# A graph layer with experts: projected rows kept as float32 and split into float32r parts on chip

## The chip, the cores and the metric

One core of a Trainium2 chip runs the whole program. The metric is device time in microseconds (us), the median of three runs. PE is the matrix engine (PEld its weight loads), DVE the vector engine, ACT the scalar engine, POOL GpSimd, SP the engine that issues most DMA transfers. Each engine takes its instructions in the order of the program that was built; engines wait for one another and for transfers by semaphores.

## What is computed

There are 6250 rows of 256 numbers and 100000 edges (`src`, `dst`), sorted by `dst`. The edges are stacked as (src, dst), so a row's neighbours are the `dst` of the edges that have it as `src`. Cut to what matters here:

```python
xn = layernorm(x)
agg = segment_sum(xn[dst], src); cnt = segment_sum(1, src)
gnn = xn @ W1.T + b1 + (agg / max(cnt, 1)) @ W2.T + b2
x = x + gnn + mix(xn)            # mix: products within 8 heads, plus xn
x = x + ffn(layernorm(x))        # each row goes to one of 8 experts
```

Since the sum over neighbours is linear, the kernel projects first, z = xn @ W2.T, and sums rows of z. This sum is the heaviest part, and the change is about how z is kept.

## The kernel before, in words

Products on PE are done in float32r, a form of float32 with fewer bits. To keep the precision, each row of z is held as two float32r parts, a high part and the remainder, and each is multiplied by itself into the same sum. Both parts are stored side by side in the DRAM tensor `z_d`: 512 numbers, 2 KB a row.

*First stage, to about 290 us.* DVE sorts the edges by `src` in many short steps (`step`, `pairs`, `last_steps`), with PE turning the data at some of them. Beside it runs `mixer`, a generator whose pieces `tick` puts between the steps of the sort, by fixed weights (`MIX`, `OWN`). For each of 49 tiles of 128 rows, a piece normalises the rows on ACT (L393), turns the next tile (L400), multiplies by `w2s` into `pz` (L421), copies the high part to `zr` as float32r (L426), multiplies it by minus one into the same `pz` so that the remainder is left there (L429), copies that to the second half of `zr` (L433), and has SP store the tile in `z_d` (L434). `zr` has three buffers. On every second tile from the seventh on, `segment` has SP load a pair of tiles of `z_d` into `z_s` (L385), twelve pairs in all. They are rows near the `dst` of each of twelve segments of the edges, and stay on chip. SP's queue thus holds stores of `z_d`, loads of `z_s` and loads of x in the order of the program.

*Second stage, from 290 us to about 1040 us.* A loop over 49 blocks `b` of 128 rows sums neighbours in `pa`. Two kinds of edges are summed:
- near edges: for each of 24 tiles of `z_s`, PE counts on chip how often a row is a neighbour (`counts`, L920: four products into `pc`), ACT casts the counts to `cn` (L923), and PE multiplies them by the tile in `z_s`. The one-hot operands `on` and `od` are made by DVE two blocks ahead (`hot_classes`, L894). Counts are two sets of four ahead of their use, and `pc` has two buffers.
- other edges, up to 1152 a block, in nine tiles of 128: POOL gathers their rows of z from `z_d` by an indirect DMA each (L910), into one of 19 buffers `zb`, and PE multiplies them by the one-hot `og`, which DVE makes a block ahead (L900). A gather into a buffer waits until PE has used it.

`add_rows` does two products each time (L823, L824): the remainder with two columns of ones, which count the edges, and the high part. A block has six steps `q`, each with four tiles of `z_s` and one or two gathered tiles; at its end `meaned` reads the sum (L970), and after every seventh block `gate_pieces` puts the gate's work in pieces between the following steps: normalising (L993), turning (L1000), `hT` (L1003), logits (L1008), choice of expert, ranks (L1043), places (L1090). It also has SP store seven tiles of rows in `buf_d` (L1074, 1.8 MB) and in `out` (L1096, 0.9 MB). Each block also loads its own x (`xt`) and y by ACT's queue and `ov` by SP's; DVE adds x and y into `row` (L960, L963). `lane_w`, an operand of L894 and L900, lies in PSUM.

*Third stage, to the end.* The experts' products (L1281, L1290), almost without a pause on PE.

There is also a loop over all edges in order (L831 on), for edges that don't fit; its number of rounds is computed, and it is zero here.

The two products, and the loop's schedule of gathered tiles:

```python
nc.tensor.matmul(ps[:, :AW], lhsT, z[:, D:], start=first, stop=False, skip_group_check=True)
nc.tensor.matmul(ps[:, :D], lhsT, z[:, :D], start=False, stop=last, skip_group_check=True)
...
t1 = GT * (j0 + 4) // J0 if j0 + 4 < J0 else GT
if not b:
    t1 = (0, 0, 2, 4, 7, GT)[q]
for t in range(t0, t1):
    add_rows(pa, og[:, t, :], zb[(b * GT + t) % NZ], not begun, False)
```

Of the kernel before, what the change touches and what calls it, by code (L numbers as in the profile page):

```python
# [16 lines left out]
P = 128  # L17
N = 6250
D = 256
NT = 49  # L20
# [3 lines left out]
DZ = 2 * D  # L24
DW = DZ + 2
# [11 lines left out]
ND = 12  # L37
# [3 lines left out]
NW = 2 * P  # L41
# [7 lines left out]
NB = NT  # L49


J0 = 2 * ND
GT = 9
# [7 lines left out]
NEC = 125  # L61
# [13 lines left out]
EPS = 1e-5  # L75
NZ = 19
OWN = 0.4
# [10 lines left out]
def gnn_mix_moe_kernel(ctx: ExitStack, tc: tile.TileContext, x, src, dst, w1t, b1g, w2t, b2g,  # L88
                       kw, kb, vw, vb, gate_w, gate_b, fw1, fb1, fw2, fb2, out):
    nc = tc.nc  # L90

    dram = ctx.enter_context(tc.tile_pool(name="dram", bufs=1, space=bass.MemoryType.DRAM))
    z_d = dram.tile([NT * P, DZ], F32, name="z_d")
    y_d = dram.tile([NT * P, D], F32, name="y_d")
# [15 lines left out]
    minus = const.tile([P, P], F32R, name="minus")  # L110
    nc.vector.tensor_scalar(minus, ident, -1.0, None, op0=OP.mult)
    ones_b = const.tile([P, P], BF16, name="ones_b")
# [50 lines left out]
    zs_ = ExitStack()  # L163
    z_p = zs_.enter_context(tc.tile_pool(name="z", bufs=1))
    z_s = z_p.tile([P, J0, DW], F32R, name="z_s")

# [11 lines left out]
    with tc.tile_pool(name="early", bufs=1) as ep, tc.tile_pool(name="work", bufs=2) as wp, \  # L178
# [199 lines left out]
        xTa = ep.tile([P, NT, 2, P], F32, name="xTa")  # L378

        def segment(i):  # L380

            _, offs = nc.values_load_multi_w_load_instructions(
                nr[0:1, i:i + 1], engines=[ET.SP], min_val=0, max_val=P if not i else NW,
                skip_runtime_bounds_check_because="it is kept in bounds")
            nc.sync.dma_start(z_s.bitcast(F32)[:, 2 * i:2 * i + 2, :DZ],  # L385
                              z_d[lo_n[i]:NW * i + 3 * P][bass.ds(offs[0], NW), :].rearrange("(j p) d -> p j d", p=P))

        def mixer():
# [19 lines left out]
            for tt in range(NT):  # L408
# [26 lines left out]
                if tt >= 6 and not tt % 2 and tt // 2 - 3 < ND:  # L435
                    segment(tt // 2 - 3)
# [392 lines left out]
    with tc.tile_pool(name="over", bufs=1) as op, \  # L829
            tc.tile_pool(name="ops", bufs=1, space=bass.MemoryType.PSUM) as pp:  # L830
        with tc.For_i(0, nit) as i:  # L831
# [12 lines left out]
            nc.vector.memset(zo.bitcast(F32)[:, DZ:], 1.0)  # L844
            nc.gpsimd.indirect_dma_start(out=zo.bitcast(F32)[:, :DZ], out_offset=None, in_=z_d,
                                         in_offset=bass.IndirectOffsetOnAxis(ap=ngb, axis=0))
            po = pp.tile([NEC, AW], F32, name="po")
            add_rows(po, eqo, zo, True, True)
# [18 lines left out]
    with tc.tile_pool(name="gather", bufs=1) as ap_, tc.tile_pool(name="gwork", bufs=2) as wp, \  # L867
# [6 lines left out]
        nc.vector.tensor_copy(lane_w, lane_b.bitcast(I32))  # L874

        zb = []
        for i in range(NZ):
            zt = ap_.tile([P, DW], F32R, name=f"zb{i}")
            nc.gpsimd.memset(zt.bitcast(F32)[:, DZ:], 1.0)
            zb.append(zt)  # L880
# [21 lines left out]

        asked, used = 0, 0

        def gathers():

            nonlocal asked
            while asked < min(used + NZ, NB * GT):
                b, t = divmod(asked, GT)
                nc.gpsimd.indirect_dma_start(  # L910
                    out=zb[asked % NZ].bitcast(F32)[:, :DZ], out_offset=None, in_=z_d,
                    in_offset=bass.IndirectOffsetOnAxis(ap=idx[:, t, b:b + 1], axis=0))
                asked += 1

        def counts(b, j0):
# [202 lines left out]

# [269 lines left out]
```

## Time and profile before

| | |
|---|---|
| median of three runs | 1362.95 us (1360.56 to 1372.96) |
| the profiled execution: its time, its span | 1377.47 us, 1375.5 us |
| busy: PE, DVE, POOL, ACT | 1108.2, 751.6, 528.9, 437.6 us |
| mean granted PE clock | 0.924 |
| DMA | 269.12 MB, mean 196 GB/s |
| of it by POOL's queue (gathers and scatters) | 134.11 MB, 31.2% of 16 engines' span |
| gathers L910 | 441, 961 ns each on POOL, 292.2 to 988.2 us |
| first and last L970 | 332.3 us, 1009.5 us |

A profile is one execution, and its durations belong to that execution, not to the median. A group's row names the line, the engine, the operation, output<-inputs, the number, then busy us and the mean ns of one, then the idle time before it and what ended most of that. A window's row gives the busy time of each engine in a stretch, with the number of instructions, the share of full clock that PE was granted, the busy share of the 16 DMA engines and GB/s. A wait row names who waited for whom. "issue" is time in which the engine waited for nothing that the profile shows.

### The profile page before, as it was taken

The page shows a single profiled execution, that of the slowest core. Times are in us where ns is not written, and L with a number is a line of the kernel's source. Part 1 is how long each engine was busy: PE and PEld are TensorE (multiplying, and loading weights), DVE is VectorE, ACT ScalarE, POOL GpSimd, SP SyncE. Part 2 cuts the span into 40 slices and gives each one's busy share as a digit, 9 for nine tenths or more (in the row PEclk, how much of TensorE's full clock was granted, in tenths as well). Part 3 has the DMA queues.
Part 4 walks back from the last instruction along what each step waited for, and adds up shares of the span by engine and source line. Part 5 has one row for each costly group of instructions (what it writes and reads, how often), then busy time and mean ns, then how long its engine had stood idle before and what let it go on. Part 6 is the DMA issues. An engine that isn't in the chain of part 4 may idle for free.

```text
span 1375.5 us, 20920 instructions
## 1 busy us (share of the span) xinstructions
PE 1108.2 (81%) x7417; PEld 995.8 (72%) x7417; DVE 751.6 (55%) x2202; ACT 437.6 (32%) x960; POOL 528.9 (38%) x580
## 2 busy tenths in 40 slices
PE   0688968736779878878789779879848999999997
PEld 0477756535778777778778778768846888888886
DVE  8998776742745554554654644544561343433434
ACT  0566833401223223323323223222432322223221
POOL 0000002046665565566666565656401222322221
PEclk9999988966999989999989989989978999999999
DMA  8665213256876886776876875865755676666750
GB/s 242 209 227 189 92 52 107 90 176 195 275 223 202 182 265 197 203 259 207 225 247 195 236 220 166 235 205 172 201 156 202 221 243 212 216 216 209 247 189 21
DMA packets 147421, 269.12 MB, mean 196 GB/s; under 512 B 18947, under 2 KB 92365, under 8 KB 147308
## 3 DMA queue, kind: packets, MB, share of 16 engines
q0 software_dynamic: 41664, 134.11, 31.2%
q1 hardware_dynamic: 75431, 105.44, 25.4%
q10 hardware_dynamic: 30213, 28.15, 6.8%
q8 instruction: 60, 0.98, 0.3%
q14 instruction: 53, 0.43, 0.1%
HBM read 216.33 MB, written 51.82 MB: 195 GB/s over the span
## 4 chain that ended last, share of the span: by engine, by line
PE 62%; issue 5%; DVE 5%; DMA 3%; another core or an unknown queue 3%; ACT 1%; POOL 0%; ACTq 0%; DVEq 0%; POOLq 0%
PE pa L823 15%; PE pa L824 13%; PE pu L1281 12%; PE pd L1290 11%; PE pc L920 7%; DMA buf_d<-row 2%; PE lgr L1008 2%; PE ph L1000 1%; ACT cn L923 1%; PE pB L1269 1%; DVE on L894 1%; DMA bt<-buf_d,idx_s 1%; DVE row L974 0%; DVE og L900 0%
## 5 line engine op out<-in xcount | busy, mean ns | idle before, releaser
L910 POOL DMA_INDIRECT zb<-z_d,idx x441 | 423.8, 961 | 273.8 <-issue 95.0
L823 PE MATMUL pa<-z_s,cn 128*128 128x258 f32 x1176 | 348.8, 324 | 12.4 <-issue 11.8
L824 PE MATMUL pa<-z_s,cn 128*128 128x256 f32 x1176 | 318.7, 298 | 13.1 <-issue 13.0
L923 ACT CAST cn<-pc 128x512 fp32r<-128x512 f32 x294 | 171.4, 586 | 445.0 <-PE pc L920 153.3
L823 PEld LDWEIGHTS pa<-z_s,cn 128*128 128x128 f32 x1176 | 242.7, 206 | 18.6 <-issue 17.9
L824 PEld LDWEIGHTS pa<-z_s,cn 128*128 128x128 f32 x1176 | 242.6, 206 | 13.9 <-issue 13.9
L894 DVE TENSOR_TENSOR on<-lane_w,nvl 128x1024 bf16<-128x1024 bf16 x147 | 101.0, 687 | 238.7 <-PE pc L920 93.3
L920 PE MATMUL pc<-od,on 128*128 128x128 bf16 x1176 | 125.7, 232 | 56.0 <-issue 31.6
L1282 ACT ACTIVATE hm<-pu,b1e 128x256 f32<-128x256 f32 (+1 forms) x192 | 88.3, 460 | 246.8 <-PE pu L1281 221.4
L1281 PE MATMUL pu<-bT,w1e 128*128 128x256 f32 (+1 forms) x768 | 163.1, 371 | 0.0
L1290 PE MATMUL pd<-w2e,hm 128*128 128x256 f32 x720 | 163.0, 379 | 0.0
L1281 PEld LDWEIGHTS pu<-bT,w1e 128*128 128x128 f32 x768 | 138.3, 192 | 24.1 <-issue 7.3
L1290 PEld LDWEIGHTS pd<-w2e,hm 128*128 128x128 f32 x720 | 134.8, 190 | 17.2
L1304 POOL DMA_INDIRECT out_dram<-lim,tki_s x45 | 45.3, 1007 | 238.8 <-DVE lim L1303 227.9
L823 PE MATMUL pa<-zb,og 128*128 128x258 f32 x441 | 129.8, 307 | 8.3 <-issue 8.2
L920 PEld LDWEIGHTS <-on 128*128 128x128 bf16 x1176 | 76.3, 103 | 76.1 <-issue 54.4
L824 PE MATMUL pa<-zb,og 128*128 128x256 f32 x441 | 124.8, 295 | 6.5 <-issue 6.4
L1293 DVE TENSOR_TENSOR yt<-pd,b2e 128x256 f32<-128x256 f32 x45 | 19.1, 424 | 180.9 <-PE pd L1290 167.4
L824 PEld LDWEIGHTS pa<-zb,og 128*128 128x128 f32 x441 | 90.3, 205 | 10.2 <-issue 10.1
L823 PEld LDWEIGHTS pa<-zb,og 128*128 128x128 f32 x441 | 90.5, 205 | 6.8 <-issue 6.7
L589 POOL DMA_INDIRECT kb<-srt_d,bi x5 | 5.2, 1043 | 204.3 <-DVE bi L585 203.1
L421 PE MATMUL pz<-w2s,xTa 128*128 128x256 f32 x196 | 56.8, 412 | 15.0 <-ACT xTa L432 14.4
(405 smaller groups left out, 1486.3 us busy)
## 6 DMA issues: line engine op xcount, KB each, us to landing
w1e<-in_fw_dram SPq DMA_DIRECT2D x24, 1024.0 KB
w2e<-in_fw_dram SPq DMA_DIRECT2D x24, 1024.0 KB
z_d<-zr SPq DMA_DIRECT2D x49, 256.0 KB
buf_d<-row SPq DMA_DIRECT2D x6, 1795.5 KB
zb<-z_d,idx POOLq DMA_INDIRECT x441
ovf_d<-zero ACTq DMA_DIRECT2D x1, 6321.0 KB
ov<-ovf_d SPq DMA_DIRECT2D x49, 129.0 KB
y_d<-xg ACTq DMA_DIRECT2D x7, 896.0 KB
```

The lines of the kernel that those rows point to most:

```text
L421: nc.tensor.matmul(pz, xT[:, c, :], w2s[:, c, :], start=(c == 0), stop=(c == 1))
L823: nc.tensor.matmul(ps[:, :AW], lhsT, z[:, D:], start=first, stop=False, skip_group_check=True)
L824: nc.tensor.matmul(ps[:, :D], lhsT, z[:, :D], start=False, stop=last, skip_group_check=True)
L894: nc.vector.tensor_tensor(to[b % 2][:, c, :].rearrange("p c (m j) -> p c m j", j=2), lanes[:, None, :w].to_broadcast([P, n, w, 2]), of.to_ ...
L910: nc.gpsimd.indirect_dma_start(out=zb[asked % NZ].bitcast(F32)[:, :DZ], out_offset=None, in_=z_d, in_offset=bass.IndirectOffsetOnAxis(ap=i ...
L920: nc.tensor.matmul(pc[:, j - j0, :], on[:, j // 2, (j % 2) * P:(j % 2 + 1) * P], od[:, j // 2, :], start=True, stop=True, skip_group_check ...
L923: nc.scalar.copy(cn[:, :n, :], pc[:, :n, :])
L1008: nc.tensor.matmul(lgp[:, t, :], hT[:, c, :], gw[:, c, :], start=(c == 0), stop=(c == 1), skip_group_check=True)
L1281: nc.tensor.matmul(pu, w1e[:, c, f * P:(f + 1) * P], bT[:, c, :q], start=(c == 0), stop=(c == 1))
L1282: nc.scalar.activation(hms[s][:, f, :q], pu, AF.Relu, bias=b1e[:, f:f + 1])
L1290: nc.tensor.matmul(pd, hm[:, f, j * P:(j + 1) * P], w2e[:, f, :], start=(f == 0), stop=(f == FC - 1))
L1304: st = nc.gpsimd.indirect_dma_start(out=out, out_offset=bass.IndirectOffsetOnAxis(ap=tki_s[:, c:c + 1], axis=0), in_=lim, in_offset=None, ...
```

## The change

z is stored as plain float32: `z_d` has 256 numbers a row, 1 KB. The projection copies `pz` once, as float32, and the product with `minus` and the second copy are gone. A new helper `in_parts` makes the two parts on chip: ACT copies to float32r (the high part), and DVE subtracts that from the float32 rows and writes the remainder.

It is used in two places. The twelve pairs of near rows are loaded to one buffer `zw`, and are split into `z_s` at the next call of `segment`, ahead of the next load. The gathers go to seven buffers `zg` of three tiles each, and each group of three is split by one ACT copy and one DVE subtraction of 768 numbers a partition, into one of three buffers `zb`. Two groups are split ahead of the loop; then one more after each group that PE has used, and the gathers that this frees are asked for. The gathered tiles are multiplied three at a time, at every second step of a block. The loop for edges that don't fit gets the same split.

```diff
+GS = 3
+NZ = 7
+NQ = 3
...
-    z_d = dram.tile([NT * P, DZ], F32, name="z_d")
+    z_d = dram.tile([NT * P, D], F32, name="z_d")
...
+    def in_parts(to, z):
+
+        nc.scalar.copy(to[:, :, :D], z)
+        nc.vector.tensor_tensor(to[:, :, D:DZ], z, to.bitcast(F32)[:, :, :D], op=OP.subtract)
...
         def segment(i):

+            while loaded:
+                n, zw = loaded.pop()
+                in_parts(z_s[:, 2 * n:2 * n + 2, :], zw)
+            if i == ND:
+                return
...
-            nc.sync.dma_start(z_s.bitcast(F32)[:, 2 * i:2 * i + 2, :DZ],
-                              z_d[lo_n[i]:NW * i + 3 * P][bass.ds(offs[0], NW), :].rearrange("(j p) d -> p j d", p=P))
+            zw = wp.tile([P, 2, D], F32, name="zw", bufs=1)
+            nc.sync.dma_start(zw, z_d[lo_n[i]:NW * i + 3 * P][bass.ds(offs[0], NW), :].rearrange(
+                "(j p) d -> p j d", p=P))
+            loaded.append((i, zw))
...
-                zr = wp.tile([P, DZ], F32R, name="zr", bufs=3)
-                nc.scalar.copy(zr[:, :D], pz)
+                zr = wp.tile([P, D], F32, name="zr", bufs=3)
+                nc.scalar.copy(zr, pz)
                 if more:
                     pT = turned(tt + 1, xn)
-                nc.tensor.matmul(pz, minus, zr[:, :D], start=False, stop=True, skip_group_check=True)
                 nc.scalar.copy(u[:, 2 * t:2 * t + 2, :], pu)
                 if more:
                     nc.scalar.copy(xTa[:, tt + 1], pT)
-                nc.scalar.copy(zr[:, D:DZ], pz)
-                nc.sync.dma_start(z_d[tt * P:(tt + 1) * P, :], zr.bitcast(F32))
-                if tt >= 6 and not tt % 2 and tt // 2 - 3 < ND:
+                nc.sync.dma_start(z_d[tt * P:(tt + 1) * P, :], zr)
+                if tt >= 6 and not tt % 2 and tt // 2 - 3 <= ND:
                     segment(tt // 2 - 3)
...
+        zg = [ap_.tile([P, GS, D], F32, name=f"zg{i}") for i in range(NZ)]
...
-            while asked < min(used + NZ, NB * GT):
+            while asked < min((parted + NZ) * GS, NB * GT):
                 b, t = divmod(asked, GT)
                 nc.gpsimd.indirect_dma_start(
-                    out=zb[asked % NZ].bitcast(F32)[:, :DZ], out_offset=None, in_=z_d,
+                    out=zg[asked // GS % NZ][:, asked % GS, :], out_offset=None, in_=z_d,
                     in_offset=bass.IndirectOffsetOnAxis(ap=idx[:, t, b:b + 1], axis=0))
                 asked += 1
+
+        def split():
+
+            nonlocal parted
+            if parted * GS < NB * GT:
+                in_parts(zb[parted % NQ], zg[parted % NZ])
+                parted += 1
+                gathers()
...
+        for _ in range(NQ - 1):
+            split()
...
-                t1 = GT * (j0 + 4) // J0 if j0 + 4 < J0 else GT
-                if not b:
-                    t1 = (0, 0, 2, 4, 7, GT)[q]
+                t1 = (((q + 1) // 2) if b else max(0, q - 2)) * GS
                 for t in range(t0, t1):
-                    add_rows(pa, og[:, t, :], zb[(b * GT + t) % NZ], not begun, False)
+                    n = b * GT + t
+                    add_rows(pa, og[:, t, :], zb[n // GS % NQ][:, n % GS, :], not begun, False)
                     begun = True
+                if t1 > t0:
+                    split()
                 t0 = t1
-                used = b * GT + t1
-                gathers()
```

More of the change, by code (lines that the diff above doesn't have):

```diff
@@ L75 @@
 EPS = 1e-5
-NZ = 19
+GS = 3
+NZ = 7
+NQ = 3
 OWN = 0.4
@@ L109, in gnn_mix_moe_kernel @@
     nc.vector.tensor_scalar(before, jp, 0.0, None, op0=OP.is_gt)
-    minus = const.tile([P, P], F32R, name="minus")
-    nc.vector.tensor_scalar(minus, ident, -1.0, None, op0=OP.mult)
     ones_b = const.tile([P, P], BF16, name="ones_b")
@@ L378, in gnn_mix_moe_kernel @@
         xTa = ep.tile([P, NT, 2, P], F32, name="xTa")
+        loaded = []
         def segment(i):
+            while loaded:
[3 more added lines that the diff above has]
+                return
             _, offs = nc.values_load_multi_w_load_instructions(
@@ L844, in gnn_mix_moe_kernel @@
             nc.vector.memset(zo.bitcast(F32)[:, DZ:], 1.0)
-            nc.gpsimd.indirect_dma_start(out=zo.bitcast(F32)[:, :DZ], out_offset=None, in_=z_d,
+            zr = op.tile([NEC, D], F32, name="zr")
+            nc.gpsimd.indirect_dma_start(out=zr, out_offset=None, in_=z_d,
                                          in_offset=bass.IndirectOffsetOnAxis(ap=ngb, axis=0))
+            nc.scalar.copy(zo[:, :D], zr)
+            nc.vector.tensor_tensor(zo[:, D:DZ], zr, zo.bitcast(F32)[:, :D], op=OP.subtract)
             po = pp.tile([NEC, AW], F32, name="po")
@@ L874, in gnn_mix_moe_kernel @@
         nc.vector.tensor_copy(lane_w, lane_b.bitcast(I32))
+        zg = [ap_.tile([P, GS, D], F32, name=f"zg{i}") for i in range(NZ)]
         zb = []
-        for i in range(NZ):
-            zt = ap_.tile([P, DW], F32R, name=f"zb{i}")
-            nc.gpsimd.memset(zt.bitcast(F32)[:, DZ:], 1.0)
+        for i in range(NQ):
+            zt = ap_.tile([P, GS, DW], F32R, name=f"zb{i}")
+            nc.gpsimd.memset(zt.bitcast(F32)[:, :, DZ:], 1.0)
             zb.append(zt)
@@ L901, in hot_gathered @@
                                     lf[:, :, b, None].to_broadcast([P, GT, P]), op=OP.is_equal)
-        asked, used = 0, 0
+        asked, parted = 0, 0
         def gathers():
             nonlocal asked
-            while asked < min(used + NZ, NB * GT):
+            while asked < min((parted + NZ) * GS, NB * GT):
                 b, t = divmod(asked, GT)
                 nc.gpsimd.indirect_dma_start(
-                    out=zb[asked % NZ].bitcast(F32)[:, :DZ], out_offset=None, in_=z_d,
+                    out=zg[asked // GS % NZ][:, asked % GS, :], out_offset=None, in_=z_d,
                     in_offset=bass.IndirectOffsetOnAxis(ap=idx[:, t, b:b + 1], axis=0))
                 asked += 1
+        def split():
[4 more added lines that the diff above has]
+                gathers()
         def counts(b, j0):
```

## The prediction

> **What bounds the kernel now.** I read the engine shares first, then the stages by windows, then single blocks of the gather loop, then who waited for whom in it. From the page and, for the sorting stage, the windows (columns: stretch, length, busy time of PE, PEld, DVE, ACT, POOL with counts, granted clock, DMA share, GB/s):
>
> ```profile
> span 1375.5 us, 20920 instructions
> ...
> PE 1108.2 (81%) x7417; PEld 995.8 (72%) x7417; DVE 751.6 (55%) x2202; ACT 437.6 (32%) x960; POOL 528.9 (38%) x580
> ...
> L910 POOL DMA_INDIRECT zb<-z_d,idx x441 | 423.8, 961 | 273.8 <-issue 95.0
> L923 ACT CAST cn<-pc 128x512 fp32r<-128x512 f32 x294 | 171.4, 586 | 445.0 <-PE pc L920 153.3
> ```
> ```profile
> 50.00:100.00 50.00, 43.47 (x261) 36.71 (x260) 46.24 (x99) 35.77 (x98) 0.00 (x0) 1.00 0.65 218
> 100.00:150.00 50.00, 42.00 (x265) 35.79 (x264) 42.76 (x103) 36.77 (x101) 0.00 (x0) 1.00 0.49 166
> ```
>
> Up to 290 us DVE sorts (46 of 50 us, 43 of 50) and the projection runs beside it on PE and ACT. The experts (1040 us to the end) are PE alone, and the change doesn't touch them. Between lies the loop over 49 blocks; its windows are cut here where a block's sum is read (L970), first the beginning, the six blocks without gate work and the rest, then one round of seven blocks:
>
> ```profile
> 292.20:332.30 40.10, 21.23 (x129) 19.12 (x129) 13.08 (x26) 4.59 (x8) 26.54 (x28) 0.65 0.73 223
> 332.30:412.30 80.00, 63.13 (x527) 59.71 (x527) 48.11 (x119) 21.11 (x36) 51.79 (x53) 0.96 0.78 243
> 412.30:1009.50 597.20, 499.66 (x4101) 471.20 (x4099) 310.51 (x886) 183.99 (x328) 345.51 (x360) 0.91 0.72 211
> ```
> ```profile
> 514.51:531.88 17.37, 11.97 (x85) 11.09 (x83) 8.21 (x22) 5.75 (x10) 9.54 (x11) 0.80 0.69 217
> 531.88:546.35 14.47, 14.07 (x132) 13.34 (x130) 5.88 (x13) 4.16 (x8) 8.49 (x9) 1.00 0.65 186
> 546.35:558.02 11.67, 10.89 (x98) 10.38 (x99) 5.79 (x13) 4.44 (x9) 7.53 (x8) 1.00 0.59 171
> 558.02:573.24 15.22, 11.92 (x105) 10.89 (x105) 10.51 (x45) 5.50 (x9) 9.30 (x11) 1.00 0.70 208
> 573.24:587.46 14.22, 11.11 (x92) 10.74 (x92) 8.59 (x23) 2.95 (x6) 7.59 (x9) 0.88 1.02 244
> 587.46:603.47 16.01, 12.77 (x98) 11.89 (x97) 8.77 (x23) 3.42 (x6) 10.32 (x11) 0.89 0.90 303
> 603.47:616.35 12.88, 11.44 (x96) 10.33 (x96) 5.79 (x14) 3.52 (x6) 8.53 (x9) 1.00 0.65 203
> ```
>
> A block takes 14.0 us in the mean, but 11.7 us where the DMA share is lowest (0.59), and 14.2 and 16.0 us where the gate's rows go to memory and the share is 0.9 to 1.0. Gate blocks (17.4, 15.2) are long for another reason: PE waits for the gate's DVE steps. No engine is busy all the time in any long block. The waits, in us in total, times, longest, between 345 and 1000 us:
>
> ```profile
> PE pc L920 <- issue: 30.9, 35, 4.2
> PE pc L920 <- ACT cn L923: 14.9, 10, 3.5
> PE pa L823 <- issue: 14.0, 26, 1.1
> PE pa L824 <- issue: 11.2, 24, 1.0
> PE ph L1000 <- DVE row L993: 8.9, 4, 3.1
> DVE row L960 <- DMA buf_d<-row: 17.0, 4, 4.7
> ```
>
> PE's pauses are many and short, and half of their time has no releaser. Some lie inside a row of products with the same operands (L824 after L823), so no operand explains them. L960 shows DMA traffic directly: DVE stands until the large store of the gate's rows has landed, and PE's L920 behind it (the 4.2 us pause at 481 us is one such). I read the loop as PE with pauses, part of which come from DMA traffic; that part is the open question.
>
> **The change part by part.**
>
> *Projection and sorting.* It removes 49 products with `minus` (L429, 384 ns) and 49 second copies (L433, 392 ns): 19 us each of PE and ACT, both beside the sort on DVE, so worth nothing on the path, though a relief for the few waits of DVE for ACT there. It adds 12 pairs for the near rows: a 128x512 ACT copy (0.59 us by L923's row, hidden beside DVE) and a 128x512 DVE subtraction. The sort's own 101x512 additions of two arrays in SBUF follow each other at 0.60 us, so 12 x 0.60 = 7.2 us, on the path, since DVE is full there. New too: DVE waits in its order for load and copy of its pair. The loads are about 6 us apart (L385, 58 to 124 us), and one buffer `zw` serves all of them: the load of pair i stands in SP's queue until the subtraction of pair i-1, and behind it stand the stores of projected rows and the loads of x. The transfer is now 256 KB, and the trace doesn't show its landing time alone: if it is under the 6 us, DVE waits for nothing; if each is late by 1.5 us, 12 x 1.5 = 18 us. I take 2 us for all, since DVE keeps its lag after the first wait. A gain is possible too: DVE waits 4.1 us for loads of x (L342), and half the store traffic goes. Sum of the stage: +9 us (ends -1 and +25).
>
> *First block.* From 303 to 320 us PE does one instruction each 0.7 us while the first 19 gathers run (DMA 0.71 to 0.73, nothing but gathers) and is quick again when they have drained; the block ends at 332.3. The changed kernel asks for 21 tiles of 128 KB. At one gather each 1.25 us (0.95 and 0.30 between) the ninth is out by 303 us, landed and split by about 307, and the block could end near 309: -23, and up to -3 for the catch-up, so -26 at most. If the stretch comes back whatever the bytes, 0. I take -15.
>
> *The loop's DMA.* Gathers fall from 115.6 to 57.8 MB, 1.18 MB a block, about 84 of the 211 GB/s. They are as many as before. Twelve blocks (two of each seven) carry the row stores: mean 15.1 us against 12.9 for the block behind them, 12 x 2.2 = 26 us; I take -20 (0 to -30). In the other 35, the unattributed pauses (L823 and L824: 43 us if each is counted from the regular step of 0.12 us) and PE's slow stretches after them may shrink: I take -20, or 0.6 us a block (0 to -43).
>
> *The loop's added work.* 147 ACT copies of 128x768: 372 ns for 256 (L426) and 586 for 512 make 0.80 us, 2.4 us a block on an engine busy 4.2 of 14. 147 DVE subtractions of 128x768: steps of 0.34 us for 256 and 0.60 for 512 make 0.86 us, 2.6 us a block, and DVE goes from 7.5 to 10.1 of 14; in the fullest block from 10.5 to 13.1 of 15.2. Both lie beside PE, and what hides them is PE's 10 us a block: without it DVE would set 10.1. The split is two groups (four sets of counts, 1.48 us each at full speed at 491 us) ahead of the products that use it, about 6 us. Each copy waits in ACT's order for three gathers, and queued behind it are the casts L923 for which PE's L920 waits; the gathers are seven groups ahead, over two blocks, so after the first block I count no wait for a landing. But every step of the gate on DVE or ACT can now stand behind a split: the PE waits on gate steps are about 45 us in 21 places; half of these longer by 0.86 us is 9 us, and the casts for 3 more: +12 us (0, if order spares them, to +34: all 21, and the 14.9 us of L923 doubled).
>
> *POOL.* 441 gathers x 1.25 us = 551 us of a loop of 717: not the bound. But a rule speaks against the change. In the trace, gathers that overlap L963 (both inputs in SBUF) take 1.06 us in the mean against 0.95 beside L894, one of whose inputs lies in PSUM: 0.11 us lost for 0.39 us of overlap. The subtraction has both inputs in SBUF. By this row 147 x 0.86 = 126 us, 59% of it beside a busy POOL, 28% of that lost: 21 us on POOL, 572 in all, hidden. The Trainium skill (SBUF — State Buffer, "SBUF: two separate sides") says more: a DVE instruction with two SBUF inputs and a GpSimd instruction that reads SBUF exclude one another for the whole instruction. By that, 9 x 1.25 + 3 x 0.86 = 13.8 us a block, and POOL would set the pace at nearly today's 14.0. I go by the row: nothing on the path.
>
> Sum: +9 - 15 - 20 - 20 + 12 = -34 us. The profiled execution took 1377.5 us (span 1375.5), 14.5 above the median of 1362.95. 1377.5 - 34 = 1343.5, less 14.5: 1329, say 1330 us.
>
> **Rivals.**
> The bytes weren't what PE waited for. For: half of PE's pause time names no DMA, and POOL's pace, the same afterwards, would explain the slow first block as well. Against: 11.7 us blocks lie where the DMA share is low. Then only +9 and +12 remain: 1384 us. It decides as soon as the three reliefs come to less than 21 us, in the loop's 49 blocks.
> The port lock works by the rule: 300 + 49 x 13.8 = 978, plus 25 for what follows the last gather, is 1003 instead of 1009.5; with +9 that is +3: 1366 us. For: gathers beside such additions are longer. Against: only by 28% of the overlap.
> DMA was the cause of all pauses outside the gate: three blocks of each seven fall to 11.7 (8.0 us, six times: -48), six early ones likewise (-10), the first by 26, +9 and +12: -63, so 1300 us.
> That the bytes don't fall can't be: the row in memory is cut to 256 numbers.
>
> **How the numbers follow.** The summed case 0.42, the full relief 0.15, the lock 0.18, the bytes that nobody waited for 0.25. A measurement of this kernel can tell about 1% from no change, 13.6 us. The first two are faster by more (0.57), the lock is within (0.18), the last slower (0.25). The low end is the full relief with the sorting stage at -1 (10 less) and half of the added waits (6 less): 1284, so 1285. The high end is the last case with 6 us more of late loads in the sorting stage: 1390. The summed case's own range is 1310 to 1349.
>
> **What would show it.** DMA share in the loop near 0.5 and the round's fifth and sixth blocks near 12.5 us would confirm the relief; if they stay at 14 and 16, it fails. The first L970 near 315 us confirms the first block. The loop's start a few us above 9 later than 290 would mean late `zw` loads, seen as DVE idle before its subtraction in the sort. Gathers at 1.0 us mean confirm the row; at 1.3 or more, the rule. PE waits for the gate's DVE rows growing by more than 12 us would make the added work dearer than I take it. I am wrong if PE's pauses without a releaser stay as they are.

## The result and the profile after

The changed kernel takes 1439.07 us (median of four, 1436.49 to 1439.89) against 1361.76 us: 1.053 of the kernel before, 95% interval 1.050 to 1.057. In the six sessions of this study (a session is what was run together, on one chip) the kernel before took 1362 to 1363 us in two and 1251 to 1264 us in four, so each ratio is taken within one session. The changed kernel is slower in both kinds: 1.052 (1.048 to 1.056) again beside 1363 us, and 1.038 (1.036 to 1.041) beside 1264 us.

From the page of the changed kernel, the span, PE and the groups that answer to those of before, with the two new ones:

```profile
span 1437.1 us, 21293 instructions
...
PE 1118.9 (78%) x7368; PEld 1001.9 (70%) x7368; DVE 868.0 (60%) x2360; ACT 539.4 (38%) x1070; POOL 564.8 (39%) x564
...
L926 POOL DMA_INDIRECT zg<-z_d,idx x441 | 459.9, 1043 | 290.3 <-issue 123.2
...
L947 ACT CAST cn<-pc 128x512 fp32r<-128x512 f32 x294 | 169.3, 586 | 220.6 <-remote 95.7
...
L167 ACT CAST zb<-zg 128x768 fp32r<-128x768 f32 x147 | 122.9, 836 | 212.4 <-PE pa L836 68.5
...
L168 DVE TENSOR_TENSOR zb<-zg,zb 128x768 fp32r<-128x768 f32 x147 | 139.6, 950 | 31.6 <-ACT zb L167 30.9
```

The gathers move half the bytes, and each takes POOL longer: 1043 against 961 ns. The sorting stage by windows (columns as before):

```profile
50.00:100.00 50.00, 39.27 (x236) 32.91 (x236) 45.53 (x92) 33.81 (x86) 0.00 (x0) 1.00 0.39 121
100.00:150.00 50.00, 40.24 (x254) 34.07 (x255) 46.90 (x116) 35.80 (x91) 0.00 (x0) 1.00 0.33 109
```

DVE is as full as it was, and DMA moves 0.6 of the bytes. The stage ends no later: the first gather starts at 288.7 us against 292.2 (287.7 against 286.4 in a second pair of traces). The loop, cut as before (first block, the six without gate work, the rest), then the same seven blocks of a round:

```profile
288.70:342.40 53.70, 20.29 (x120) 19.27 (x121) 17.68 (x31) 9.77 (x15) 35.84 (x36) 0.57 0.38 118
342.40:424.60 82.20, 65.93 (x523) 61.81 (x522) 52.55 (x109) 33.05 (x52) 53.17 (x52) 0.91 0.37 111
424.60:1070.30 645.70, 516.68 (x4115) 482.98 (x4114) 411.03 (x1037) 275.35 (x453) 370.90 (x354) 0.87 0.45 125
```
```profile
519.27:547.56 28.29, 18.39 (x104) 15.56 (x103) 9.81 (x23) 8.14 (x13) 15.67 (x16) 0.64 0.42 128
547.56:559.81 12.25, 11.08 (x103) 10.53 (x102) 9.31 (x21) 5.97 (x11) 9.29 (x9) 1.00 0.35 103
559.81:582.12 22.31, 14.35 (x104) 13.81 (x104) 9.55 (x21) 6.64 (x12) 11.89 (x13) 0.77 0.33 98
582.12:595.44 13.32, 13.32 (x128) 12.91 (x127) 10.21 (x33) 9.39 (x15) 5.69 (x6) 1.00 0.35 103
595.44:608.24 12.80, 10.31 (x99) 9.60 (x99) 12.78 (x42) 5.50 (x9) 8.46 (x8) 1.00 0.80 151
608.24:616.81 8.57, 8.57 (x82) 8.39 (x81) 8.57 (x20) 5.00 (x8) 5.89 (x6) 1.00 0.95 239
616.81:630.39 13.58, 10.34 (x90) 9.54 (x89) 8.75 (x19) 4.75 (x7) 10.69 (x10) 1.00 0.42 126
```

The DMA share falls from 0.72 to 0.45, and the two blocks with the row stores do shrink, from 14.2 and 16.0 us to 12.8 and 8.6 (8.57 us with DVE busy throughout is the shortest block of this trace). But the first and the third block grow to 28.3 and 22.3 us, and the round from 101.8 to 111.1 us. The difference of the two spans, 61.6 us, is: start of the gathers -3.5, first block +13.6 (53.7 against 40.1), 48 further blocks +50.7 (727.9 against 677.2), what follows +0.8. The waits between 345 and 1065 us:

```profile
DVE rs L1010 <- ACT rs L1009: 61.2, 7, 18.2
PE pc L944 <- ACT cn L947: 45.8, 36, 5.6
PE lgr L1032 <- ACT hT L1027: 26.5, 11, 7.3
PE pc L944 <- issue: 25.8, 21, 3.3
PE pa L836 <- issue: 17.1, 29, 1.7
PE pa L835 <- issue: 11.6, 25, 1.3
PE ph L1024 <- DVE row L1017: 2.3, 3, 1.2
```

PE's pauses without a releaser are what they were: with 4.7 us at L1032 they make 59.2 us, against 60.2 before. New are its waits for ACT, for count casts above all. The largest wait of the list is DVE's, for the gate's root that ACT makes behind casts and copies; it is tested below, since a large wait is not yet a loss (a second trace of the changed kernel has 25.3 us of it in place of 61.2, in nearly the same time).

### The profile page after: what moved, and what is told of

It reads as the page before. It is cut to its first block, busy times and chain, and to the rows that moved or that the text cites. A ratio compares the mean times of both kernels' runs of the same rounds, so it can differ in the third digit from the quotient of the medians.

```text
span 1437.1 us, 21293 instructions
## 1 busy us (share of the span) xinstructions
PE 1118.9 (78%) x7368; PEld 1001.9 (70%) x7368; DVE 868.0 (60%) x2360; ACT 539.4 (38%) x1070; POOL 564.8 (39%) x564
## 4 chain that ended last, share of the span: by engine, by line
PE 52%; another core or an unknown queue 10%; DVE 9%; issue 5%; DMA 4%; ACT 4%; POOL 2%; ACTq 1%; DVEq 0%; POOLq 0%
PE pu L1306 11%; PE pd L1315 11%; PE pa L835 10%; PE pa L836 9%; PE pc L944 5%; DMA zg<-z_d,idx 2%; PE lgr L1032 2%; PE pz L461 2%; POOL zg L926 2%; ACT cn L947 1%; DVE zb L168 1%; ACT zb L167 1%; PE ph L1024 1%; DVE on L910 1%
## 5 line engine op out<-in xcount | busy, mean ns | idle before, releaser
L926 POOL DMA_INDIRECT zg<-z_d,idx x441 | 459.9, 1043 | 290.3 <-issue 123.2
L836 PE MATMUL pa<-z_s,cn 128*128 128x256 f32 x1176 | 323.3, 301 | 15.1 <-issue 14.6
L836 PEld LDWEIGHTS pa<-z_s,cn 128*128 128x128 f32 x1176 | 246.3, 209 | 15.3 <-issue 14.9
L835 PEld LDWEIGHTS pa<-z_s,cn 128*128 128x128 f32 x1176 | 246.4, 210 | 12.6 <-issue 12.3
L167 ACT CAST zb<-zg 128x768 fp32r<-128x768 f32 x147 | 122.9, 836 | 212.4 <-PE pa L836 68.5
L944 PEld LDWEIGHTS <-on 128*128 128x128 bf16 x1176 | 81.1, 106 | 132.6 <-issue 112.7
L168 DVE TENSOR_TENSOR zb<-zg,zb 128x768 fp32r<-128x768 f32 x147 | 139.6, 950 | 31.6 <-ACT zb L167 30.9
L910 DVE TENSOR_TENSOR on<-lane_w,nvl 128x1024 bf16<-128x1024 bf16 x147 | 100.3, 682 | 71.0 <-remote 35.7
L835 PEld LDWEIGHTS pa<-zb,og 128*128 128x128 f32 x441 | 93.7, 212 | 11.1 <-issue 6.4
L836 PEld LDWEIGHTS pa<-zb,og 128*128 128x128 f32 x441 | 93.8, 213 | 5.4 <-issue 5.4
```

The costliest lines, as they stand in the source:

```text
L167: nc.scalar.copy(to[:, :, :D], z)
L168: nc.vector.tensor_tensor(to[:, :, D:DZ], z, to.bitcast(F32)[:, :, :D], op=OP.subtract)
L910: nc.vector.tensor_tensor(to[b % 2][:, c, :].rearrange("p c (m j) -> p c m j", j=2), lanes[:, None, :w].to_broadcast([P, n, w, 2]), of.to_ ...
L926: nc.gpsimd.indirect_dma_start(out=zg[asked // GS % NZ][:, asked % GS, :], out_offset=None, in_=z_d, in_offset=bass.IndirectOffsetOnAxis(a ...
L944: nc.tensor.matmul(pc[:, j - j0, :], on[:, j // 2, (j % 2) * P:(j % 2 + 1) * P], od[:, j // 2, :], start=True, stop=True, skip_group_check ...
```

## The experiments

The theory at the start was: the splits cost more than the halved bytes give, because copies and subtractions stand in ACT's and DVE's queues ahead of count casts and gate steps. Its rivals were the order of three gathered tiles in a row, and the effect of the two-operand subtraction on POOL.

**Without the split (e1).** Gathers go straight into operand tiles, of which there are seven:

```diff
...
-                    out=zg[asked // GS % NZ][:, asked % GS, :], out_offset=None, in_=z_d,
+                    out=zb[asked // GS % NQ].bitcast(F32)[:, asked % GS, :D], out_offset=None, in_=z_d,
...
-                in_parts(zb[parted % NQ], zg[parted % NZ])
```

> The changed kernel with the split of the gathered rows left out of the loop: each 1 KB row is gathered straight into the first half of the operand tile, and its second half (the remainder) stays zero, so that the products of the gathered rows miss the remainder. The near rows are split as in the changed kernel. Seven groups of three tiles instead of seven and three. Theory A (the copies and subtractions cost what was lost, because they stand in ACT's and DVE's queues ahead of the count casts and the gate): the time falls from 1439 to 1300 to 1345 us, under the kernel before. Rival B (the loss is in the order of three gathered tiles in a row or in the 1 KB gathers themselves): 1400 us or more. Rival C (the split is the loss, but bytes were never waited for): 1350 to 1385 us, the time of the kernel before.

Measured: 0.9997 (0.998 to 1.001) of the kernel before, at 1253 us. This is rival C: beside 1253 us half the bytes are worth nothing, and all of the loss is the split. The same kernel was run three times more, to meet the kernel before at 1363 us, and never did:

> The changed kernel without the split of the gathered rows, as before (gathered rows lack their remainder), again, because the kernel before took 1253 us in the session of the first four runs and 1363 us in the others, and TensorE there made almost none of the pauses inside runs of products (2 to 4 us against 30 to 52 us). If the kernel before takes near 1363 us: theory S (the splits in the two in-order queues are the whole loss, and half the bytes are worth nothing in either session): 0.985 to 1.01 of the kernel before. Rival R (the pauses go with the bytes, so that halving them gains where they are long, and the splits cost more than what is seen): 0.94 to 0.975. If it takes near 1253 us: 1.00 as before.

> The changed kernel without the split of the gathered rows (they lack their remainder). If the kernel before takes near 1363 us, which no run of this kernel has met yet: theory S (half the bytes are worth nothing there too, the split is the whole loss): 0.985 to 1.01 of the kernel before. Rival R (the bytes gain there, and the split costs more than 5 per cent): 0.94 to 0.975. If it takes near 1252 us: 1.00 a third time.

> The changed kernel without the split of the gathered rows (they lack their remainder), a fourth time, for the case that the kernel before takes near 1363 us. Then theory S (half the bytes are worth nothing, the split is the whole loss): 0.985 to 1.01 of the kernel before. Rival R (the bytes gain there, and the split costs more than 5 per cent): 0.94 to 0.975. If it takes near 1255 us: 1.00.

Measured: 1.0015, 1.0009 and 0.9999, intervals of 0.2% about each, all beside 1251 to 1264 us. The products of gathered rows stand in threes here too, so that costs nothing there either. What half the bytes are worth beside 1363 us, no run shows.

**What the split waits for (e2, e9), where its copy runs (e3), and the gate's root (e4).** The edits are other numbers of tiles for e2 and e9, a tensor_copy on DVE for e3, and a first guess by integer shift with three Newton steps for e4:

```diff
-NZ = 7
-NQ = 3
+NZ = 5
+NQ = 5
```
```diff
-NQ = 3
+NQ = 4
```
```diff
-                in_parts(zb[parted % NQ], zg[parted % NZ])
+                in_parts(zb[parted % NQ], zg[parted % NZ], nc.vector.tensor_copy)
```
```diff
-            nc.scalar.activation(rs[:, :n], mv[:, :n, 1], AF.Sqrt, bias=eps)
-            nc.vector.reciprocal(rs[:, :n], rs[:, :n])
...
+            nc.vector.tensor_scalar(rs.bitcast(I32)[:, :n], ri, -1.0, float(0x5F3759DF), op0=OP.mult, op1=OP.add)
+            for _ in range(3):
...
```

> The changed kernel with five operand tiles and five gathered groups in place of three and seven, so that a split may run four groups ahead of its products instead of two. In the trace of the changed kernel ACT's copies waited 68 us for products of gathered rows and 43 us for counts. Theory A1 (a copy that waits for an operand tile to come free holds up the count cast behind it in ACT's queue): 1415 us or less. Rival A2 (it is the splits' own 0.84 and 0.95 us in the two queues, not the tiles they wait for): 1430 to 1448 us.

> The changed kernel with four operand tiles for split groups instead of three, all else the same (seven gathered groups), so that a copy waits for the products three groups back and not two. In the changed kernel ACT's copies waited 65 us for products of gathered rows, 47 us for counts and 60 us for what the trace does not tell. Theory W (the copy waits for its operand tile, with count casts behind it): the time falls by 1.5 per cent or more of the kernel before, PE's waits for count casts from 52 us to under 35 us. Rival X (the tile is only one of the copy's waits; the work in the queue is the loss): within 0.7 per cent of the changed kernel's 1.052.

> The changed kernel with the copy of each gathered group made by DVE instead of ACT; the sort stage keeps its copies on ACT. Theory A-ACT (the loss is count casts and the gate's root standing behind copies in ACT's queue): ACT's queue is as before, PE waits for count casts under 20 us instead of 46, and the time is 1380 to 1415 us although DVE gets 147 x 0.5 to 0.95 us = 75 to 140 us more. Rival A-DVE (DVE's order sets the pace: blocks of 8.6 us with DVE busy throughout are the fastest there are): 1450 to 1520 us.

> The changed kernel with the copy of each gathered group made by DVE, again. If the kernel before takes near 1363 us: theory Q-ACT: 1.00 to 1.03 of the kernel before, because ACT's queue holds only what it held before and a count cast no longer waits behind a copy; PE waits for count casts under 25 us (52 us in the changed kernel). Rival Q-DVE: 1.055 or more, DVE having 147 x 0.95 = 140 us more to do. Near 1253 us: 1.043 as before.

> The changed kernel with the gate's root made on DVE by a first guess and three Newton steps (15 small instructions of 0.1 to 0.2 us for each of 9 gates, some 2 us each), so that DVE does not wait for ACT's root any more, and ACT loads one function table less. In the trace of the changed kernel DVE stood 61 us in 7 waits for that root, up to 18 us at a time, against 1.8 us before. Theory D (these waits are on the path: all that stands behind them on DVE, split, class tiles and gate, is late by them): 1385 to 1415 us. Rival E (PE is slow in those stretches for another reason, and DVE would have waited for PE anyway): 1430 to 1448 us.

Measured, all beside 1251 to 1253 us: five tiles 1.044 (1.039 to 1.048), four tiles 1.043 (1.040 to 1.046), copy on DVE 1.043 twice (1.040 to 1.047), root on DVE 1.035 (1.031 to 1.038). Against the changed kernel's 1.038 of another session of this kind none gains more than 0.3%. So neither the operand tile that a copy waits for nor the wait for the root is the loss there. Without ACT's copies and with 139 us more on DVE the time is nearly the same, although the gathers took 1.115 us in the mean here, so e3 alone doesn't clear ACT's queue; the next runs do. What all four share is the subtraction.

**Copies alone (e8) and a subtraction turned into a copy (e5).**

```diff
-                in_parts(zb[parted % NQ], zg[parted % NZ])
+                in_parts(zb[parted % NQ], zg[parted % NZ], False)
...
-        nc.vector.tensor_tensor(to[:, :, D:DZ], z, to.bitcast(F32)[:, :, :D], op=OP.subtract)
+        if rest:
+            nc.vector.tensor_tensor(to[:, :, D:DZ], z, to.bitcast(F32)[:, :, :D], op=OP.subtract)
```

For e5 an `else:` follows with `nc.vector.tensor_copy(to[:, :, D:DZ], z)`.

> The changed kernel with ACT's copy of each gathered group kept and DVE's subtraction left out (the remainder of the gathered rows stays zero). Theory Q-ACT (count casts that stand behind a copy that waits in ACT's queue are the larger loss): 1.025 to 1.05 of the kernel before, near the changed kernel. Rival Q-DVE (the subtraction, its 0.95 us in DVE's queue and its effect on POOL, is the larger loss): within 0.01 of the kernel without a split. A session near 1253 us: the gathers' mean of 0.96 to 0.98 us again, and the kernel without a split plus less than 1 per cent.

> The changed kernel with ACT's copies kept and DVE's subtraction left out (gathered rows lack their remainder). If the kernel before takes near 1363 us: theory Q-DVE (the subtraction is the loss, by its place in DVE's queue and on POOL): within 1.2 per cent of the kernel without a split of this call. Rival Q-ACT (count casts behind copies): 1.03 to 1.05 of the kernel before. If near 1252 us: 1.004 again.

> The changed kernel with DVE's subtraction replaced by a copy of the same elements from one SBUF operand (the operand tile's second half holds the row and not its remainder). If the kernel before takes near 1252 us: theory G (the second operand slows POOL's gathers, and they are the bound): the gathers' mean 0.96 to 0.99 us and 1.00 to 1.015 of the kernel before. Rival H (DVE's 0.95 us and the waits are the loss): 1.035 to 1.05. If near 1363 us: 1.047 again.

> The changed kernel, unchanged, beside the variants of this call. If the kernel before takes near 1252 us: theory G (there POOL's gathers follow one another without a pause, so that what lengthens a gather lengthens the loop): 1.035 to 1.05 of the kernel before, 441 x 0.09 to 0.11 us = 40 to 48 us, as the variants with three, four and five operand tiles. If it takes near 1363 us: 1.052 again.

Measured in one session beside 1264 us: changed kernel 1.038, copies alone 1.003 (1.001 to 1.005; 1.004 in the first run), one-operand copy on DVE 1.006 (1.004 to 1.008), without the split 1.001. The gathers' rows (busy us, mean ns, idle before them), first of the changed kernel, then with the one-operand copy, then with copies alone, then without a split, all of that session:

```profile
L926 POOL DMA_INDIRECT zg<-z_d,idx x441 | 472.2, 1071 | 158.5 <-issue 112.9 <-DMA zg<-z_d,idx 27.3 <-DVE zb L168 3.7
```
```profile
L929 POOL DMA_INDIRECT zg<-z_d,idx x441 | 428.0, 971 | 163.5 <-issue 90.2 <-DMA zg<-z_d,idx 34.9 <-ACT cn L950 9.1
```
```profile
L928 POOL DMA_INDIRECT zg<-z_d,idx x441 | 427.2, 969 | 161.4 <-issue 108.0 <-DMA zg<-z_d,idx 33.3 <-ACT cn L949 13.7
```
```profile
L926 POOL DMA_INDIRECT zb<-z_d,idx x441 | 426.8, 968 | 164.0 <-issue 64.8 <-PE pa L836 46.8 <-PE pc L943 26.2
```

Idle time is 158 to 164 us in all four, 0.36 to 0.37 us behind each gather: POOL goes from one to the next. Only the first has longer gathers, by 44 to 45 us in all, and 1313.6 - 1270.8 = 43 us is what the subtraction costs over a copy of the same length (947 ns each) in the same place and queue. By the overlap of single instructions: of the changed kernel's gathers, the 142 that meet a subtraction for 0.3 us or more take 1.27 us, the other 299 0.98; with the one-operand copy the 147 that meet it take 0.970, the rest 0.971.

The mean of 1.27 us hides two kinds of gathers. From the timeline of the changed kernel in that session (start, us), two subtractions and two gathers:

```profile
498.72 0.95 DVE L168 TENSOR_TENSOR zb<-zg,zb 128x768 fp32r<-128x768 f32 x1
499.00 1.49 POOL L926 DMA_INDIRECT zg<-z_d,idx  x1 [0.30 <-issue]
500.79 0.95 POOL L926 DMA_INDIRECT zg<-z_d,idx  x1 [0.30 <-issue]
501.30 0.94 DVE L168 TENSOR_TENSOR zb<-zg,zb 128x768 fp32r<-128x768 f32 x1
```

The first gather begins while a subtraction runs, and ends 0.82 us after it; the second has begun before its subtraction and takes the usual 0.95. So it is throughout: of the 99 gathers that begin during a subtraction, 82 end 0.81 to 0.83 us after its end, however long it still had to run, and the 99 together take 43 us more than 0.946 us each, nearly all of the 44 to 45. Of the 91 that begin before one, 84 take under 1.0 us, and no subtraction takes over 1.03 us. The 102 gathers that begin during the one-operand copy take 0.948 us, none over 0.952. The 38 of the changed kernel that begin during L910, two operands of which one lies in PSUM, and meet no subtraction, take 0.946. So it is two operands in SBUF, not DVE's time: a gather that begins during such an instruction waits for its end.

**What bounds the kernel before at 1252 us.** The changed kernel's larger time there follows from longer gathers if gathers set the pace of the kernel before:

> The kernel before, unchanged, for its trace beside the others. If it takes near 1255 us: theory G: over 420 of its 441 gathers begin within 0.33 us of the end of the one before (325 at 1366 us), and its loop, from the first gather to the last addition of a mean, is 441 x (0.96 + 0.33) = 570 us and what lies behind the last gather. Rival H (products or waits for bytes set its pace): fewer than 380. If it takes near 1363 us: as in its other trace.

Measured: 1251.5 us; 432 of 441 gathers begin within 0.33 us of the end of the one before. Its gathers, then its loop by windows (first block, 48 blocks), then the one wait of PE in its list (310 to 880 us):

```profile
L910 POOL DMA_INDIRECT zb<-z_d,idx x441 | 424.1, 962 | 157.0 <-issue 54.1 <-DMA zb<-z_d,idx 53.2 <-PE pa L824 23.8
```
```profile
292.00:308.20 16.20, 13.28 (x100) 12.75 (x100) 12.99 (x27) 4.60 (x8) 12.29 (x13) 0.74 0.87 281
308.20:882.60 574.40, 522.73 (x4656) 501.77 (x4654) 358.45 (x1003) 206.73 (x364) 411.73 (x428) 0.94 0.85 260
```
```profile
PE pa L823 <- DMA zb<-z_d,idx: 51.4, 17, 8.2
```

At a DMA share of 0.85, above the 0.73 of the trace at 1376 us, PE has no pause without a releaser in the list, and the first block takes 16.2 us instead of 40.1. The same kernel moved the same bytes, faster: the bytes alone don't make the pauses and the slow start. PE waits for gathers, and these come at POOL's pace, 441 x (0.962 + 0.356) = 581 us. In the changed kernel at 1313 us two of the waits in the loop (320 to 940 us) are:

```profile
PE pc L944 <- ACT cn L947: 97.4, 29, 15.1
ACT zb L167 <- DMA zg<-z_d,idx: 140.7, 39, 16.7
```

A late gather now holds a copy, and the count cast behind that copy holds PE: products of near rows, which need no gather, wait too. That chain is not itself the loss here: with copies alone it stands as well (PE waits 71.5 us for count casts, ACT's copies 134.5 us for gathers, between 310 and 900 us), and costs 0.3%.

**Where the kernel before takes 1363 us.** The kernel before with 147 subtractions that nobody reads (e7), and e5 in that session:

```diff
+                if q in (1, 3, 4):
+                    nc.vector.tensor_tensor(spare, z_s.bitcast(F32)[:, :3, :D], z_s.bitcast(F32)[:, 3:6, :D], op=OP.subtract)
```

> The kernel before with three subtractions of 128x768 float32 added to DVE's queue in each block, 147 in all, from two stretches of the near rows into a spare tile that nobody reads; gathers of 2 KB rows, no split, nothing waits for them but what stands behind them on DVE (busy 3 x 0.95 us more of a block of some 12 to 14). Theory G: the gathers' mean rises by 0.07 to 0.11 us and the time by 2.5 to 4.5 per cent, though no product needs the result. Rival H (what is lost is lost by waits for the split): under 1 per cent.

> The changed kernel with DVE's subtraction in the loop replaced by a plain copy of the same 128x768 float32 elements to the same place (the second half of the operand tile then holds the row itself and not its remainder). All instructions, queues and waits stay in number and place; the copy took 0.945 us against the subtraction's 0.949 in an earlier run, so DVE is as busy, but it reads one SBUF operand and not two. Theory G (the two-operand read slows POOL): the gathers' mean falls to 0.95 to 0.99 us and the time to within 1 per cent of the kernel before. Rival H (the work and the waits in ACT's and DVE's queues are the loss): the time stays at 1.035 to 1.055 of the kernel before.

> The kernel before, unchanged, for its trace beside the others. Theory G (the loop is bound by the pace of POOL's gathers where TensorE does not pause): if the time is near 1253 us, over 420 of the 441 gathers begin within 0.33 us of the end of the one before (323 of 441 in its first trace, which took 1377 us), and the steps of products longer than 0.3 us inside a run without waits, 30 us there, are under 5 us. Rival H (another resource bounds it): fewer than 380 of 441 follow so closely.

> The changed kernel, unchanged, for its trace and its ratio beside the others. Theory G (a subtraction that reads two SBUF operands lengthens a gather that overlaps it from 0.98 to about 1.27 us, and gathers set the loop's pace): 1.035 to 1.06 of the kernel before; the gathers' mean is 1.03 to 1.09 us against 0.96, and 441 times the difference, 30 to 55 us, is most of what the loop loses. Rival H (the copies standing in ACT's queue are the loss): the loop loses more than twice what the gathers' mean explains, and POOL waits for split groups to free its tiles.

Measured: subtractions alone 1.013 (1.009 to 1.017); one-operand copy 1.047 (1.042 to 1.051); changed kernel 1.052; the kernel before 1367 us with 325 gathers close behind one another. Theory G fails here. The gathers of e7, then of e5, then of the changed kernel:

```profile
L911 POOL DMA_INDIRECT zb<-z_d,idx x441 | 477.5, 1083 | 216.2 <-issue 91.9 <-PE pc L921 45.0 <-PE pa L824 33.8
```
```profile
L929 POOL DMA_INDIRECT zg<-z_d,idx x441 | 426.0, 966 | 317.7 <-issue 128.8 <-ACT zb L167 74.3 <-ACT cn L950 63.6
```
```profile
L926 POOL DMA_INDIRECT zg<-z_d,idx x441 | 467.1, 1059 | 278.6 <-issue 119.7 <-DVE zb L168 83.5 <-ACT cn L947 25.4
```

53 us more on POOL cost 19 us. 41 us less gave 5.5 us, which the intervals (1.042 to 1.051 against 1.048 to 1.056) don't tell from nothing. So POOL has slack there, and most of the 5.2% is lost elsewhere.

Where, can be worked out from the starts of PE's instructions in the 48 blocks behind the first; counted as lost is what a step from one start to the next has beyond 0.12 us, when it is over 0.3 us. The regular product steps make 432 to 436 us in two traces of the kernel before and two of the changed kernel. The time lost before counts grows from 51 to 52 us to 79 to 85, that inside runs of products from 44 to 45 to 60 to 64, that before the gate's products falls from 42 to 45 to 22 to 38, and the first block is 14 us longer. With the one-operand copy (e5) the first two are 68 and 72 us and the first block takes 55.0 us, as in the changed kernel; with the subtractions that nobody reads (e7) they are 44 and 31, and the first block takes 38.4. So these losses come with what e5 has and e7 has not: copies between gather and product, groups of three, 1 KB rows. In the faster sessions all of that together costs 0.6% (e5 there); here none of it was tried apart. Which part it is stays open, and so does any gain by bytes, as no run without the split met such a session.

Lower clock is not the cause by itself: 318 to 335 regular product steps fall in stretches where the profile shows half the clock granted, against 274 to 277 in the kernel before, and each takes 0.21 us there instead of 0.13. That is 4 to 5 us. Whether the longer pauses there have to do with the clock (113 to 119 us of the 48 blocks at half clock before, 184 to 198 after) is not told apart.

## Why the prediction was wrong

It said 1330 us, 1285 to 1390, and faster; the time is 1439. Two steps failed. The relief by fewer bytes (-15 and -40) did not come: PE's pauses without a releaser stayed at 59 us, and beside 1251 to 1264 us the kernel with half the bytes and no split takes 1.000 to 1.0015 of the time. And the split (+12 for added work, nothing for POOL) cost more: beside 1264 us its subtraction alone made 43 us through POOL's gathers, and in the trace of the result PE's waits for casts and gate steps grew by 47 us.

*Projection and sorting, +9.* The 12 subtractions took 688 ns each, 8.3 us (7.2 were counted), with 1.7 us of waits (2), yet the stage's end moved by -3.5 and +1.3 us in the two pairs of traces. The step was reckoned some 9 us too dear; what paid for the subtractions is not told apart.

*First block, -15.* It became +13.6. The premise was that PE is slow while gathers run because of what they move; the same block with the same bytes takes 16.2 us in a faster session.

*The loop's DMA, -40.* This is the step that failed first. The DMA share fell as said, and the fifth and sixth blocks shrank as said, but PE's pauses without a releaser stayed at 59 us, which the text had named as what would prove it wrong. A likelier reading of the 11.7 us blocks is 9 x (0.96 + 0.30) = 11.3 us, POOL's pace for nine gathers: at 1252 us the three blocks ahead of the longest, in each round but the first, take 10.8 to 11.5 us with 2 KB rows and 10.8 to 11.4 with 1 KB rows. That reading of the blocks at 1376 us is argued, not shown. One possible sign of relief is in the traces at 1363 us: PE's steps of over 0.3 us inside runs of products at full clock fell from 37 to 41 us in all to 30 to 32. Those at half clock grew from 14 to 19 us to 46 to 48.

*Added work, +12.* The mechanism, casts and gate steps behind splits, shows in the waits where the time is 1363 us; the size was wrong. PE's waits for count casts grew from 14.9 to 45.8 us and for ACT's gate copies from 4.0 to 26.5, for the gate's rows they fell from 8.9 to 2.3: +47 us. The text had counted the wait for a landing as nothing after the first block and asked how often a step would stand behind one split; it did not ask what a split itself waits for, which then everything in the queue waits for (ACT's copies wait 68.5 us for the products that free their tile, 43.4 for counts and 19.0 for gathers in this trace). That these waits are the loss, and not only stand beside it, is not shown.

*POOL, nothing on the path.* The row said 28% of an overlap with L963 lost, 21 us in all, and hidden. Measured: 36 us in the trace of the result (441 x 0.082), 44 to 45 us at 1264 us. The row was a mean over two kinds of gathers. In the trace of before, too, 11 of the 14 gathers that begin while L963 runs end 0.81 to 0.82 us after its end. What such a gather loses is what is left of the DVE instruction when it begins, less some 0.13 us, so the loss grows faster than the instruction: L963 runs 0.42 us, the subtraction 0.95. With a gather each 1.33 us an estimate from these figures is 147 x (0.95 - 0.13) / 1.33 x 0.41 = 37 us.

The rule of the Trainium skill (SBUF — State Buffer, "SBUF: two separate sides") is that of a DVE instruction with two SBUF inputs and a GpSimd instruction that reads SBUF, whichever starts first holds the shared ports for its whole length and the other waits. For a gather that begins second the traces agree, and with the condition too (two inputs in SBUF, not one). For a gather that begins first they don't: the subtraction runs beside it and takes 1.03 us at most instead of 0.95. The prediction's sum by the rule, 13.8 us a block, added both whole lengths and so was too dear; at 1264 us the changed kernel took 629.7/48 = 13.1, and the kernel without the split 584.9/48 = 12.2.

The hiding place depends on the session. The prediction compared POOL's 551 us with the loop's 717 and took the gaps of the 1376 us trace for slack. Where the kernel before takes 1363 us that holds for the most part (53 us more on POOL cost 19). Where PE doesn't pause there is no slack, and 44 us of longer gathers made 43 us of time.

*Rivals.* "The bytes weren't what PE waited for", at 0.25, named the right direction, and at 1252 us it is shown; its time, 1384, carried the +12 with it and so fell short by 55 us.

## What to carry to other kernels

Before a share (DMA at 0.7 beside short and long blocks) is read as a cause, look for a trace with the same bytes and other times, or make one: leaving the split out while halving the bytes showed in one run that, beside 1253 us, they are worth nothing. Price a DVE instruction with two SBUF operands beside a stream of gathers by who begins first: a gather that begins during it waits for its end, one that began before loses nothing, so by this reading one long instruction costs more than short ones of the same total with room between them (no run tried that). Ask whether POOL's gaps are waits for somebody or only the 0.33 us between two gathers. For a step put into an in-order queue, ask what it waits for, not only what it takes (0.84 us here): everything behind it waits as well.

## What the runs showed of the hardware

The same program took 1362 to 1363 us in two sessions and 1251 to 1264 us in four. The experts take the same (366 to 367 us from the last sum to the end) and the sort nearly; the loop differs, 40 us for the first block and 673 to 677 for the others against 16 and 574. In the slower sessions PE makes 95 and 98 steps of over 0.3 us inside runs of products that wait for nothing the profile shows (131 and 134 in the changed kernel), up to 22 of them over 1 us; in the faster ones every kernel makes 13 to 28, none over 1 us. Their cause was not found. The record names the chip of five sessions: chip 4 for a slower one, chips 2, 3 (twice) and 13 for the faster ones. No chip was seen in both kinds, so a difference between chips is not ruled out.

A DVE copy with one SBUF operand, float32 to float32r, 128x768 in 947 ns, leaves a gather beside it at 0.970 us, as do ACT's copies (0.969). A subtraction of the same length with both operands in SBUF holds a gather that begins during it: the gather ends 0.82 us after the subtraction, up to 2.0 us long, while one that began first takes 0.95 us.
